# A four-layer macaron network: layer 1 as one run over the token chunks, and row sums by chunk

## The chip, the core and the metric

One Trainium2 chip, one NeuronCore. The metric is the device time of one execution in microseconds (us), the median of several runs. Instructions run on five engines that take their own queues in order: PE (TensorE matmul), DVE (VectorE), ACT (ScalarE), POOL (GpSimd) and SP (SyncE, which here issues DMAs). All arithmetic is float32.

## What is computed

The input x has B = 2 rows of S = 512 tokens with D = 256 features. Four layers follow each other, and each is a half-weighted FFN, an attention-like mixer and the same half-weighted FFN again. `LN` is a layer norm without weights.

```
for L in (0, 1, 2, 3):
    x = x + 0.5 * ffn_L(LN(x))
    x = x + attn_L(LN(x))
    x = x + 0.5 * ffn_L(LN(x))
```

The FFNs of layers 0 and 3 are mixtures of experts (layer 0 picks 6 of 32 for each token). Layer 1's FFN is one 256 x 256 product with a binarized weight and a bias. Layer 1's mixer is a sparse attention with 16 heads of 16:

```
importance = x @ Wi + bi                    # one number for each token
mask = (importance > its 103rd largest in the row) or (token is among the 32 most important)
q = x @ Wq + bq;  k = (x @ Wk + bk) * mask;  v = (x @ Wv + bv) * mask
out = softmax(q k^T / 4) v,  then  out @ Wo + bo
```

Layer 0's mixer is a retention network, and those of layers 2 and 3 are state-space (Mamba) blocks.

## The kernel before

The 1024 tokens are NC = 8 chunks of P = 128. x stays in SBUF for the whole program as `self.x[:, c, :]`, 128 tokens by 256 features a chunk; chunks 0 to 3 are row b = 0, chunks 4 to 7 row b = 1 (CB = 4 chunks a row). KD = 2 is the number of 128-feature halves. A product needs tokens along the free axis, so each norm ends in PE transposes through PSUM and a copy by DVE or ACT.

**Order.** Most stages are plain loops whose instructions a scheduler then places on each engine; the order on an engine is fixed before the program runs. In the Mamba blocks `in_order` (near L140) ties the instructions of PE, ACT and DVE to the order in which the code calls the pieces.

**Sums that are left over.** A mixture of experts writes each token's K expert outputs to a DRAM array and does not add them itself. `add_rows` (L637 to L651) brings them back, a pair of chunks in one `y2` buffer, and adds: for K = 6 one DVE addition of 128x768 (L648) and three of 128x256 (L651). It is stored as `pending[b]`, and whoever reads x first calls `settle(b)` (L155), which adds all four chunks of the row. `moments(b)` (L172 to L179) calls it and then takes mean and variance of the four chunks on DVE (`bn_stats` L178, `bn_aggr` L179). `scales` (L184 to L188) makes 1/sqrt(var + eps) for four chunks on POOL: an addition (L187) and a power (L188), each on a 128x4 tile. `layernorm` (L193) applies it on DVE, chunk by chunk.

**Layer 0's mixer** (the loop that begins at L978): eight chunks go through a software pipeline, `norm`, `project`, `turn`, `scores`, `values` and so on. `scales(b)` there (L735 to L743) makes two factors for a row by two powers of 128x4.

**Layer 1** is three stages.

- `l1_ffn` (L1030 to L1045), for each row: `row(b)` norms and transposes the row, DVE adds the bias (L1038, 128x1024), PE makes `ps_y` (L1042, two matmuls of 128x256 a chunk), and DVE adds it to x (L1045).
- `l1_attn`: POOL makes the tables `before` (L1081, used to break ties between ranks), `weight` (L1095, L1096) and clears `va` (L1100). `norm(0)`, `importance(0)` (`ib`, L1119), `ranks` (L1134 to L1140), `places` (L1145 to L1149), `norm(1)`, then keys and values of the picked tokens. Then comes a loop over n = 0 to 15 half-chunks: `scores` (PE `ps_s` L1253; DVE `mx` L1257 and `p` L1259; ACT's exponential L1260), `turn` (PE transposes `ps_t` L1268), `values` (PE `po` L1281), `finish` (`pt_o` L1295, `den`, `o`), and `project` (PE `pt2` L1309, ACT copy `oT2` L1311, POOL adds the bias `bo` to x L1313, PE `pw` L1316, DVE adds `pw` to x L1317). The loop's PSUM pool `a1n` has one buffer of each tag; `pt2` and `pw` share the tag `mm`.
- `l1_ffn` again for both rows.

**The Mamba blocks** (`mamba`, L1840 ff. for the opening that the change touches) begin with `row(0)`, the decay sums `d0`, `d1` (`pd`, `dt`, `dA`, `ps_row`, `cr`), the convolution's taps on DVE (L1584) and the `silu` on ACT (L1588), then the first chunks' exponents.

Of the kernel before, what the change touches and what calls it, by code (L numbers as in the profile page):

```python
# [32 lines left out]
def _const_array():  # L33
# [11 lines left out]
        "icol": np.arange(NC)[None, :] * P + p,  # L45
        "own": (p // 16 % 2 == np.arange(2)[None, :]),
# [33 lines left out]
class Net:  # L80
# [74 lines left out]
    def settle(self, b):  # L155
        if b in self.pending:
            self.pending.pop(b)()
# [6 lines left out]
    def transpose_tokens(self, src, dst, psum, half, k):  # L164

        ps = psum.tile([P, S], F32, tag="mm", name="ps_tr")
        for j in range(CB):
            self.nc.tensor.transpose(ps[:, j * P : (j + 1) * P], src[:, j, k * P : (k + 1) * P], self.ident)  # L168
        self.evac(dst[:, k, half * S : (half + 1) * S], ps)

# [32 lines left out]
    def layernorm_T(self, es, psum):  # L203
# [16 lines left out]
        def row(b):  # L220
            measure(b)
            norm(b)
            for k in range(KD):
                turn(b, k)

# [344 lines left out]
    def moe(self, pre, names, E, F, K, FS, PER, tiles, cap, r, scores, scale):  # L570
# [69 lines left out]
        def add_rows(b):  # L640
            for c0 in range(b * CB, (b + 1) * CB, 2):
                y2 = self.w("y2")[:, : 2 * K * D].rearrange("p (c n d) -> p c n d", c=2, n=K)
                for i in range(2):
                    nc.sync.dma_start(y2[:, i], rv[c0 + i, :, :K, :])
                for i in range(2):
                    y, xc, n = y2[:, i], self.x[:, c0 + i, :], K
                    if n == 6:
                        nc.vector.tensor_tensor(y[:, 0:3], y[:, 0:3], y[:, 3:6], ALU.add)  # L648
                        n = 3
                    for j in range(n):  # L650
                        nc.vector.tensor_tensor(xc, xc, y[:, j], ALU.add)  # L651

        for b in range(B):
            self.pending[b] = partial(add_rows, b)
# [49 lines left out]
    def l0_attn(self):  # L704
# [10 lines left out]
        with ExitStack() as es:  # L715
# [14 lines left out]
            rstd = sb.tile([P, NC], F32, name="ln_rstd")  # L730
            rr = sb.tile([P, NC], F32, name="ln_rr")
# [3 lines left out]
            def scales(b):  # L735
                bs = slice(b * CB, (b + 1) * CB)
                mv = mvs[b] = self.moments(sb, b)
                var = mv[:, :, 1]
                nc.gpsimd.tensor_scalar(rr[:, bs], var, 1.0 + EPS, EPS * EPS, ALU.mult, ALU.add)
                nc.gpsimd.tensor_tensor(rr[:, bs], rr[:, bs], half[:, :CB], ALU.pow)  # L740
                nc.gpsimd.tensor_scalar(rstd[:, bs], var, EPS, None, ALU.add)
                nc.gpsimd.tensor_tensor(rstd[:, bs], rstd[:, bs], half[:, :CB], ALU.pow)
                nc.vector.scalar_tensor_tensor(nb[:, bs], mv[:, :, 0], -1.0, rstd[:, bs], ALU.mult, ALU.mult)  # L743
# [16 lines left out]
            def norm(c):  # L760
                hn = wk.tile([P, D], F32, tag="hn", name="hn")
                nc.vector.tensor_scalar(
                    hn, self.x[:, c, :], mvs[c // CB][:, c % CB, 0:1], rr[:, c : c + 1], ALU.subtract, ALU.mult
                )
                nc.scalar.activation(
                    h0[:, c, :], self.x[:, c, :], AF.Identity, bias=nb[:, c : c + 1], scale=rstd[:, c : c + 1]
# [204 lines left out]
            scales(0)  # L971
            norm(0)
            scales(1)
# [4 lines left out]
            for s in range(NC + 4):  # L978
                if 0 <= s - 2 < NC:
                    scores(s - 2)  # L980
                if s + 1 < NC:
                    norm(s + 1)
# [23 lines left out]
    def l1_ffn_ahead(self):  # L1006
# [3 lines left out]
        self.hb = self.row("L1_ffn_bias")  # L1010
        with tc.tile_pool(name="f1p", bufs=1) as sb, tc.tile_pool(name="f1pm", bufs=2, space=PSUM) as psM:
# [18 lines left out]
    def l1_ffn(self):  # L1030
        nc, tc = self.nc, self.tc
        with ExitStack() as es:
            psM = es.enter_context(tc.tile_pool(name="f1m", bufs=8, space=PSUM))
            xT, row, measure, norm, turn = self.layernorm_T(es, psM)
            for b in range(B):
                row(b)
                xb = self.x[:, b * CB : (b + 1) * CB, :]
                nc.vector.tensor_tensor(xb, xb, self.hb.unsqueeze(1).to_broadcast([P, CB, D]), ALU.add)  # L1038
                for c in range(b * CB, (b + 1) * CB):
                    ps = psM.tile([P, D], F32, tag="mm", name="ps_y")  # L1040
                    for k in range(KD):
                        nc.tensor.matmul(  # L1042
                            ps, xT[:, k, c * P : (c + 1) * P], self.bwT[:, k, :], start=(k == 0), stop=(k == KD - 1)
                        )
                    nc.vector.tensor_tensor(self.x[:, c, :], self.x[:, c, :], ps, ALU.add)  # L1045


    def l1_attn(self):
# [15 lines left out]
        with ExitStack() as es:  # L1064
# [4 lines left out]
            wt = self.w("w4")[:, : KD * 4 * D].rearrange("p (k n d) -> p k n d", k=KD, n=4)  # L1069
            for n, name in enumerate(("Wq", "Wk", "Wv", "Wo")):  # L1070
                nc.sync.dma_start(wt[:, :, n, :], a[pre + name].rearrange("(k p) d -> p k d", p=P))
            wi = sb.tile([P, KD, 1], F32, name="wi")
            nc.sync.dma_start(wi, a[pre + "Wi"].rearrange("(k p) o -> p k o", p=P))
            bq, bk = self.col(pre + "bq", D), self.col(pre + "bk", D)
            bv, bo, bi = self.row(pre + "bv"), self.row(pre + "bo"), self.row(pre + "bi", 1)
            wib = sb.tile([P, KD, P], F32, name="wib")
            nc.gpsimd.tensor_copy(wib, wi.to_broadcast([P, KD, P]))

            before = sb.tile([P, CB, S], F32, name="before")
            for cc in range(CB):  # L1080
                nc.gpsimd.tensor_scalar(  # L1081
                    before[:, cc, :], self.c["jrow"], self.c["icol"][:, cc : cc + 1], None, ALU.is_lt
                )
# [9 lines left out]

            weight = sb.tile([P, 1], F32, name="weight")
            nc.gpsimd.tensor_scalar(weight, self.c["icol"][:, 0:1], P - 1.0, float(S - P), ALU.is_equal, ALU.mult)  # L1095
            nc.gpsimd.tensor_scalar(weight, weight, 1.0, None, ALU.add)  # L1096
            vas, kbs, ibs = [], [], {}
            for b in range(B):
                vas.append(sb.tile([P, NH, HQ], F32, name=f"va{b}"))
                nc.gpsimd.memset(vas[b], 0.0)  # L1100
                nc.gpsimd.tensor_copy(vas[b][:, :, DH : DH + 1], weight.unsqueeze(1).to_broadcast([P, NH, 1]))
                kbs.append(sb.tile([P, KD, 2, P], F32, name=f"kb{b}"))

            def norm(b):
                xr = xn[:, b * CB : (b + 1) * CB, :]
                self.layernorm(sb, xr, b, *self.scales(sb, b))
                for k in range(KD):
                    self.transpose_tokens(xr, xT, psM, b, k)
# [20 lines left out]
            def ranks(b, cc):  # L1129
# [8 lines left out]
                nc.vector.scalar_tensor_tensor(t, ib, me, before[:, cc, :], ALU.is_equal, ALU.mult)  # L1138
# [88 lines left out]
            bqs = sb.tile([P, KD], F32, name="bqs")  # L1227
            nc.vector.tensor_scalar(bqs, bq, DH**-0.5, None, ALU.mult)
            with tc.tile_pool(name="a1m", bufs=4, space=PSUM) as psM:
                norm(0)  # L1230
                importance(0)
                for cc in range(CB):
                    ranks(0, cc)
# [230 lines left out]
    def mamba(self, pre, win, wout, nh):  # L1464
# [14 lines left out]
        with ExitStack() as es:  # L1479
# [359 lines left out]
            with self.in_order(tail, ("PE", "Activation", "DVE")):  # L1839
# [6 lines left out]
                if few:  # L1846
                    measure(1)
# [174 lines left out]
```

## Time and profile before

| what | value |
|---|---|
| median of 3 runs | 2051.31 us (2039.61 to 2053.77) |
| the profiled execution's own time | 2134.34 us |
| its span, first to last instruction | 2132.1 us, mean granted PE clock 0.901 |
| busy share of the span | PE 83%, DVE 54%, POOL 41%, ACT 37% |
| layer 1 in the span | about 740 to 925 us |

The stages found from the timeline, in us from the start of the span: layer 0's first FFN to 288, its mixer to 455, its second FFN to 735; layer 1 to 925; layer 2 to 1240; layer 3 from there, with its mixer's sums read in from 1358 and its second FFN from 1993, to 2132. The page's list of costly groups is led by the experts and the Mamba blocks, which the change does not enter; so this case is read by windows and by the timeline, not by the list. In a timeline line the columns are the start in us, the time in us, the engine, line, operation and tiles, how many instructions the line holds, and in brackets how long the engine had been idle and what ended that.

### The profile page before, as it was taken

The numbers are of one execution on the slowest core, as the hardware profiler recorded it, in microseconds if no ns is written. First come the engines' busy times: TensorE is split into PE (matmuls) and PEld (weight loads), VectorE is DVE, ScalarE is ACT, GpSimd is POOL, SyncE is SP. The second block draws the span as 40 slices with busy tenths as digits, with TensorE's granted clock in tenths as the row PEclk, the third lists the DMA queues.
The fourth block names the chain that finished last, engine by engine and source line by source line (L and its number), as shares of the span: only waits on it lengthen the run. The fifth ranks groups of instructions, "written<-read, shape, count | busy, mean of one in ns | idle before, by whom it ended". The sixth has DMA issues, their size and how long they took to land. (4 is left out here: it accounts for less than half of the span.)

```text
span 2132.1 us, 29472 instructions
## 1 busy us (share of the span) xinstructions
PE 1772.7 (83%) x10590; PEld 1258.1 (59%) x10590; DVE 1144.8 (54%) x2679; ACT 798.5 (37%) x1329; POOL 879.1 (41%) x821
## 2 busy tenths in 40 slices
PE   6898849898888737879687988569999999999885
PEld 4576626565666524554366456447777677777564
DVE  5432256316322268656564653377777767776533
ACT  1122214311122204510562012267877677777111
POOL 3466545330666430000042016124566537667253
PEclk8999969998999858979697989789999999999788
DMA  8255450040455340000221013243444444544132
GB/s 286 78 163 157 138 207 12 1 149 24 137 163 159 115 173 1 1 21 0 90 91 31 10 30 96 95 133 119 154 148 149 159 137 154 165 142 128 41 92 91
DMA packets 117438, 226.00 MB, mean 106 GB/s; under 512 B 22382, under 2 KB 68828, under 8 KB 117142
## 3 DMA queue, kind: packets, MB, share of 16 engines
q1 hardware_dynamic: 88134, 170.17, 24.6%
q0 software_dynamic: 20608, 48.45, 7.0%
q10 hardware_dynamic: 8528, 5.26, 0.8%
q8 instruction: 92, 1.51, 0.3%
q14 instruction: 76, 0.62, 0.1%
HBM read 195.13 MB, written 41.81 MB: 111 GB/s over the span
## 5 line engine op out<-in xcount | busy, mean ns | idle before, releaser
L475 POOL DMA_INDIRECT xe<-table,sl_get x176 | 179.8, 1022 | 228.5 <-DVE sl_get L451 146.7
L499 PE MATMUL ps_gu<-we,xeT 128*128 128x352 f32 x704 | 238.1, 481 | 0.0
L529 POOL DMA_INDIRECT rows<-ye,sl_put x176 | 177.0, 1005 | 139.7 <-ACT ye L128 45.6
L524 PE MATMUL ps_ye<-we,hT 88*128 88x256 f32 x704 | 178.6, 396 | 40.7 <-issue 14.1
L1584 DVE SCALAR_TENSOR_TENSOR xc<-pp,L_attn_cols,xc 128x511 f32<-128x511 f32 (+2 forms) x216 | 161.4, 747 | 48.5 <-ACT xc L1580 43.2
L524 PEld LDWEIGHTS ps_ye<-we,hT 88*128 88x128 f32 x704 | 134.7, 195 | 86.7 <-issue 19.6
L504 DVE SCALAR_TENSOR_TENSOR he<-se,xe,ps_gu 128x176 f32<-128x176 f32 x176 | 68.4, 396 | 208.4 <-issue 106.7
L499 PEld LDWEIGHTS ps_gu<-we,xeT 128*128 128x128 f32 x704 | 133.8, 202 | 59.3 <-issue 10.3
L187 POOL TENSOR_SCALAR ln_rstd<-ln_mv 128x4 f32<-128x4 f32 x22 | 5.1, 234 | 393.9 <-DVE ln_mv L179 389.4
L1711 PE MATMUL pz<-xT,wt 128*128 128x128 f32 x1152 | 145.1, 280 | 19.5 <-DVE state L1758 8.0
L1687 DVE SCALAR_TENSOR_TENSOR lm<-lm,jb,top 128x128 f32<-128x128 f32 x576 | 153.6, 340 | 0.0
L1711 PEld LDWEIGHTS pz<-xT,wt 128*128 128x128 f32 x1152 | 137.7, 195 | 25.2 <-issue 9.3
L1577 PE MATMUL pp<-xT,wx 128*128 128x512 f32 x288 | 145.2, 629 | 1.5 <-ACT dec L1568 0.9
L1784 PE MATMUL yacc<-wt,y 128*128 128x256 f32 x576 | 144.1, 393 | 0.7 <-POOL y L1766 0.7
L1766 POOL TENSOR_TENSOR y<-y,sg 128x512 f32<-128x512 f32 x72 | 91.7, 1274 | 108.4 <-DVE y L1765 107.1
L1704 POOL TENSOR_TENSOR ce<-ce,CT 128x1024 f32<-128x1024 f32 x54 | 128.0, 2370 | 0.0
L128 ACT COPY xT<-ps_tr 128x512 f32<-128x512 f32 x22 | 12.8, 584 | 293.4 <-PE ps_tr L168 264.9
L503 ACT ACTIVATE se<-ps_gu 128x176 f32<-128x176 f32 x176 | 54.7, 318 | 172.9 <-PE ps_gu L499 75.8
L1784 PEld LDWEIGHTS yacc<-wt,y 128*128 128x128 f32 x576 | 104.6, 191 | 24.1 <-issue 10.6
L1416 PE MATMUL ps_y<-w8T,xT 128*128 128x512 f32 x256 | 118.5, 617 | 0.0
L1739 PE MATMUL py<-lm,xt 128*64 128x128 f32 x1152 | 109.2, 284 | 6.2 <-issue 5.4
L168 PE MATMUL ps_tr<-cst,xn 128*128 128x128 f32 x176 | 41.9, 394 | 86.5 <-DVE xn L193 67.0
(383 smaller groups left out, 3552.4 us busy)
## 6 DMA issues: line engine op xcount, KB each, us to landing
lm<-rows SPq DMA_DIRECT2D x72, 512.0 KB
ce<-rows SPq DMA_DIRECT2D x54, 512.0 KB
rows<-zero POOLq DMA_DIRECT2D x16, 768.0 KB
y<-rows SPq DMA_DIRECT2D x16, 768.0 KB
we<-in_L_ffn_w_gate_dram SPq DMA_DIRECT2D x64, 176.0 KB
we<-in_L_ffn_w_up_dram SPq DMA_DIRECT2D x64, 176.0 KB
we<-in_L_ffn_w_down_dram SPq DMA_DIRECT2D x64, 176.0 KB
we<-in_L_ffn_w_dram SPq DMA_DIRECT2D x48, 176.0 KB
```

What stands on the lines that cost most here:

```text
L475: nc.gpsimd.indirect_dma_start(xe[:, i, :], None, table, bass.IndirectOffsetOnAxis(get[:, e * per + j : e * per + j + 1], 0), bounds_check ...
L499: nc.tensor.matmul(pg, xeT[:, k, i * P : (i + 1) * P], wgu[:, :, k], start=(k == 0), stop=(k == KD - 1))
L524: nc.tensor.matmul(py[:, i, :], hT[:, q, i * P : (i + 1) * P], wd[:, q, :], start=(q == 0), stop=(q == 1))
L529: put_rows = nc.gpsimd.indirect_dma_start(rows, bass.IndirectOffsetOnAxis(put[:, e * per + j : e * per + j + 1], 0), y[:, i, :], None, bou ...
L1416: nc.tensor.matmul(ps, xT[:, k, cs], self.w8T[:, k, 2 * e2 : 2 * e2 + 2, :], start=(k == 0), stop=(k == KD - 1))
L1577: nc.tensor.matmul(pp, wv[:, k, :], xT[:, k, b * S : (b + 1) * S], start=(k == 0), stop=(k == KD - 1))
L1584: nc.vector.scalar_tensor_tensor(out[:, 3 - w :], pp[:, : S - 3 + w], cw[:, m, w : w + 1], out[:, 3 - w :], ALU.mult, ALU.add)
L1687: nc.vector.scalar_tensor_tensor(k["lm"][:, h, :], k["lm"][:, h, :], jb[:, k["c"], n : n + 1], top, ALU.add, ALU.min)
L1704: nc.gpsimd.tensor_tensor(k["ce"], k["ce"], ct, ALU.mult)
L1711: nc.tensor.matmul(pz[:, m, :], u["wz"][:, kk, m * P : (m + 1) * P], xT[:, kk, c * P : (c + 1) * P], start=(kk == 0), stop=(kk == KD - 1),)
L1739: nc.tensor.matmul(py[i * HP : (i + 1) * HP, m, :], w[:, h * HP : (h + 1) * HP], v[:, h, :], start=(m == 0 and n == 0), stop=(n == len(src ...
L1784: nc.tensor.matmul(yacc[cc // 2][:, cc % 2, :], k["y"][:, m, :], u["wo"][:, m, :], start=(u["g"] == 0 and m == 0 and cc % 2 == 0), stop=(u ...
```

## The change

1. **Sums by chunk.** `pending[b]` is a list of four parts, and `settle(b, n)` adds the first n of them. The first part issues the DMAs of all four chunks. If a PSUM pool is handed over, a chunk's six pieces are added by six PE products with the identity into `ps_add`, and DVE adds that once.
2. **Layer 0's mixer** makes its factors by chunk (`scales(c)`), two chunks ahead of the loop, with one power of 128x2 instead of two of 128x4. The rest are made in the loop.
3. **Layer 1 is one function `l1`.** A first loop takes chunk c through `front` (sum, mean and variance, power of 128x1), chunk c-1 through `turn_x` (norm, transposes, ACT copy, bias on POOL), c-2 through `back` (the FFN's product and addition), c-3 through `measure` and c-4 through attention's `norm` (whose POOL part now adds `bo`). `importance(0)`, `queries(0)` and `ranks(0)` follow in its last steps. In the attention loop, `front`, `turn_x` and `back` of the second FFN run some steps behind `project`, in the same one-buffer PSUM tag `mm`. `before` and `weight` become columns of the constants array that is loaded at the start, and Layer 1's small vectors are loaded ahead, in layer 0.
4. **The Mamba openings**: `row(b)` of a row with sums still to add goes chunk by chunk (`by_chunks`); the calls of `d0`, `d1`, the taps and `silu` of the first units stand in another order; in layer 3 the norm of row 1 comes one step later.
5. **The store** adds a chunk's sums ahead of that chunk's DMA.

```diff
-        def add_rows(b):
...
+        def add_rows(b, cc, psum):
+            c, pair = b * CB + cc, cc // 2
+            if cc == 0:
...
+            if psum:
+                ps = psum.tile([P, D], F32, tag="mm", name="ps_add")
+                for j in range(n):
+                    nc.tensor.matmul(ps, self.ident, y[:, j], start=(j == 0), stop=(j == n - 1))
+                nc.vector.tensor_tensor(xc, xc, ps, ALU.add)
+                return
...
+    def scale(self, pool, name, c):
+        mv = self.moment(pool, name, c)
+        rstd = pool.tile([P, 1], F32, name=f"ln_rs{name}")
+        nc.gpsimd.tensor_scalar(rstd, mv[:, 1:2], EPS, None, ALU.add)
+        nc.gpsimd.tensor_tensor(rstd, rstd, self.mhalf[:, 0:1], ALU.pow)
+        return mv, rstd
...
+            def front(c):
+                self.settle(c // CB, c % CB + 1, psM if c % 2 or c >= CB else None)
+                ms[c] = self.scale(sb, f"{nth}_{c}", c)
+            def turn_x(c):
+                fx = self.centre(sb.tile([P, D], F32, tag="fxn", name="fxn", bufs=3), c, *ms.pop(c))
+                pt = psM.tile([P, KD, P], F32, tag="mm", name="pt")
+                for k in range(KD):
+                    nc.tensor.transpose(pt[:, k, :], fx[:, k * P : (k + 1) * P], self.ident)
+                xts[c] = sb.tile([P, KD, P], F32, tag="fxT", name="fxT", bufs=3)
+                nc.scalar.copy(xts[c], pt)
+                nc.gpsimd.tensor_tensor(self.x[:, c, :], self.x[:, c, :], self.hb, ALU.add)
+            def back(c):
+                xT = xts.pop(c)
+                ps = psM.tile([P, D], F32, tag="mm", name="ps_y")
+                for k in range(KD):
+                    nc.tensor.matmul(ps, xT[:, k, :], self.bwT[:, k, :], start=(k == 0), stop=(k == KD - 1))
+                nc.vector.tensor_tensor(self.x[:, c, :], self.x[:, c, :], ps, ALU.add)
...
             with tc.tile_pool(name="a1m", bufs=4, space=PSUM) as psM:
-                norm(0)
-                importance(0)
-                for cc in range(CB):
-                    ranks(0, cc)
+                for c in range(NC + 4):
+                    if c < NC:
+                        front(c)
...
+                    if 0 <= c - 1 < NC:
+                        turn_x(c - 1)
+                    if 0 <= c - 2 < NC:
+                        back(c - 2)
+                    if 0 <= c - 3 < NC:
+                        measure(c - 3)
+                    if c >= 4:
+                        norm(c - 4)
...
                 if n >= 4 and n % 2 == 0 and (n - 4) // 2 < NC:
                     project((n - 4) // 2)
+                if n >= 5 and n % 2:
+                    if (n - 5) // 2 < NC:
+                        front((n - 5) // 2)
+                    if 0 <= (n - 7) // 2 < NC:
+                        turn_x((n - 7) // 2)
+                if n >= 8 and n % 2 == 0 and (n - 8) // 2 < NC:
+                    back((n - 8) // 2)
...
                 exponents(ks[0])
                 x[2][0]()
+                x[2][1]()
...
                 raised(ks[0])
-                x[2][1]()
```

## The prediction

> **What bounds the kernel now.** I read the page first. PE leads:
>
> ```profile
> PE 1772.7 (83%) x10590; PEld 1258.1 (59%) x10590; DVE 1144.8 (54%) x2679; ACT 798.5 (37%) x1329; POOL 879.1 (41%) x821
> ```
>
> An average of 83% says nothing of the stages that the change touches, so I cut the span into windows around them. Columns: length, then busy us (instructions) of PE, PE's weight loads, DVE, ACT and POOL, the granted PE clock, the DMA share, GB/s. The windows are the opening of layer 0's mixer, its steps, layer 1's first FFN, its attention steps and its second FFN.
>
> ```profile
> 290.00:305.00 15.00, 0.00 (x0) 0.00 (x0) 11.59 (x27) 0.00 (x0) 4.53 (x13) 0.50 1.00 389
> 305.00:455.00 150.00, 130.27 (x960) 84.41 (x961) 70.48 (x183) 52.88 (x128) 73.34 (x80) 0.92 0.18 60
> 745.00:785.00 40.00, 16.93 (x48) 12.59 (x48) 29.13 (x70) 1.17 (x2) 3.35 (x5) 0.56 0.67 241
> 843.00:901.00 58.00, 50.18 (x502) 32.82 (x502) 38.72 (x52) 33.42 (x53) 0.00 (x0) 0.97 0.01 1
> 901.00:926.00 25.00, 15.18 (x62) 11.77 (x62) 17.50 (x57) 1.83 (x4) 3.79 (x6) 0.80 0.13 43
> ```
>
> Both FFNs of layer 1 leave PE idle about half the time, at a clock of 0.56 in the first; attention's steps keep it 87% busy. What PE waits for stands in the timeline of DVE:
>
> ```profile
> 794.29 2.20 DVE L193 TENSOR_SCALAR xn<-x,ln_mv,ln_rstd 128x256 f32<-128x256 f32 x4 [6.66 <-POOL ln_rstd L188]
> ...
> 801.43 0.74 DVE L1119 TENSOR_SCALAR ib<-pb,row_L_attn_bi 128x512 f32<-128x512 f32 x1
> ...
> 825.57 1.22 DVE L1257 TENSOR_REDUCE mx<-ps_s 128x8 f32<-128x1024 f32 x1
> ...
> 867.69 0.42 DVE L1317 TENSOR_TENSOR x<-x,pw 128x256 f32<-128x256 f32 x1 [1.24 <-PE pw L1316]
> ...
> 875.75 0.42 DVE L1317 TENSOR_TENSOR x<-x,pw 128x256 f32<-128x256 f32 x1 [1.23 <-PE pw L1316]
> ...
> 924.27 0.41 DVE L1045 TENSOR_TENSOR x<-x,ps_y 128x256 f32<-128x256 f32 x1
> ```
>
> The first importance comes at 801.43, 56.5 us after the first sum (744.98); the first scores at 825.57; a chunk of attention takes 8.06 us; the second FFN ends 19.3 us after the last `pw` (905.42). The 6.66 us idle is POOL, which builds a table before it takes the norm:
>
> ```profile
> 784.31 6.19 POOL L1081 TENSOR_SCALAR before<-cst 128x512 f32<-128x512 f32 x4 [10.23 <-PE ps_y L1042]
> ...
> 793.22 1.04 POOL L188 TENSOR_TENSOR ln_rstd<-ln_rstd,mhalf 128x4 f32<-128x4 f32 x1
> ```
>
> The openings of layers 0, 3 and 2 have the same look: first norm after all four chunks' sums (layer 0's first sum was at 292.84, layer 3's sums ended at 1365.15), and PE without work behind ACT:
>
> ```profile
> 307.59 0.41 DVE L762 TENSOR_SCALAR hn<-x,ln_mv,ln_rr 128x256 f32<-128x256 f32 x1
> ...
> 1369.09 1.38 DVE L193 TENSOR_SCALAR xn<-x,ln_mv,ln_rstd 128x256 f32<-128x256 f32 x4 [1.54 <-POOL ln_rstd L188]
> ```
> ```profile
> 1062.17 1.11 PE L1659 MATMUL pt<-cst,xc 128*128 128x128 f32 x4 [10.23 <-ACT xc L1588]
> ```
>
> **What the Trainium skill says.** "Perfetto Trace Analysis", Optimizing Scalar/DVE Operations: if those engines aren't saturated but cause bubbles elsewhere, breaking up instructions may let work finish sooner. That is this change, and DVE at 54% with PE waiting fits. "GPSIMD Engine Reference", 4.1: GpSimd is about twice as slow as VectorE for a two-input operation; the trace has `bo`'s addition at 0.74 us on POOL against 0.42 on DVE. "TensorE: Matmul & The Clock Gate", Part 1: the array runs at half rate unless it has been busy; 16 matmuls of `ps_y` took 6.64 us at 777 and 3.72 us at 920, so 0.42 against 0.23 each. "ScalarE: Activation LUTs", What ACT_TABLE_LOAD costs: about 1.28 us and a drain; the trace shows the 1.28.
>
> **The change part by part**, against the profiled execution (2134.3 us; the runs' median is 3.9% lower, so the sum is scaled by 0.961 at the end).
>
> *Front of layer 1.* The y pieces arrive 2.1 us apart as before. In the steady step DVE does: add `ps_add` 0.42, statistics 0.43, aggregate 0.17, add `ps_y` 0.42, norm 0.35, statistics 0.43, aggregate 0.17, norm 0.35 = 2.74. Each norm waits for POOL's addition 0.22 and power. No 128x1 power is in the trace. I split 1.04 for 128x4 into 0.22 fixed and 0.205 a column: 0.42 (bounds 0.22 and 1.04). With handoffs of 0.2 a wait is 0.84; the first is half covered by adding `ps_y` (0.42 left), the second is open and has 0.2 more, because POOL first adds the FFN's bias (0.73). Step 2.74 + 0.42 + 1.04, and 0.15 for POOL's `bo`: 4.4 us. PE fits beside it: six identity products at the cold 0.42 are 2.5, transposes and `ps_y` some 1.9. The first norm is at about 749.3 (744.98, sum 2.3, statistics 0.6, wait 0.84, and the next chunk's work between); 7.4 steps later, at 782, stands importance: -19.4. With a power of 1.04 the step is 5.6, and it is -11. The table on POOL is gone. From importance to the first scores it was 24.1, and stays that and 0.7 for chunk 7's leftovers: first scores 807, -18.7.
>
> *Attention's steps.* The chunk is a ring: `x+=pw`, `mx`, `p`, exponential, `ps_t`, `po`, `pt2`, `pw`. DVE's queue now has, between `x+=pw` and the next `mx`, statistics 0.43, aggregate 0.17, the wait 0.84, norm 0.35, and `ps_y` 0.42, less the overlaps in the trace: `mx` starts 2.75 after `x+=pw` instead of 0.67. Behind them stand `mx`, and PE's `ps_t`. So +2.05 a chunk, six chunks, less in the first two: +11.6; +3.6 more at 1.04. The two small PE pieces (transposes 0.44, `ps_y` 0.5) run in the time that `mx` is awaited; without that cover they cost about 1 a chunk.
>
> *Second FFN.* 19.3 us after the last `pw` become 4.8 (one norm, transposes, copy, product, addition), and 1.3 for the last `pw`: -13.2.
>
> Layer 1: -18.7 + 11.6 - 13.2 = -20.3. Bounds: -7 (power 1.04), -25 (0.22).
>
> *Layer 0's mixer.* Chunk 0's mean and variance are there at 296.9 as before (its sum, statistics and aggregate behind 292.84); POOL then needs 0.32 + 0.23 for two additions and, by my split, 0.63 for one power of two columns: first norm at 298.2, not 307.59: -9.4. The remaining sums, 2.3 each, go into steps where DVE is 47% busy; a part will be late. The second row's y DMAs move on SP behind `fc1` and `fc2`, needed only four steps on. I take -7.5 (0 to -9.4).
>
> *Mamba openings.* Layer 3: statistics and norm of three chunks go under the sums; first transposes done about 3.4 earlier, and `cr` before the taps. Layer 2: one 1.28 table load less on ACT, the bubble of 10.23 shrinks. Bounds 0 and -5 for layer 2, +2 and -8 for layer 3 (its row 1 norm is a step later); I take -3 and -5.
>
> *Start.* The constants grow from 717 KB by 897 columns, 448 KB, beside x's load at about 385 GB/s: +1.2, as the first statistics wait for x (8.30). Ahead loads of small vectors: nothing, hidden under layer 0's experts. *Store*: the same order as before, 0.
>
> Sum: -20.3 - 7.5 - 3 - 5 + 1.2 = -34.6; times 0.961, -33: 2018 us.
>
> **Rivals.**
>
> *A: the power does not shrink with its columns* (a 128x1 costs 1.04). [...] Against: additions of 128x4 and 128x1 (0.22 to 0.25) show a small fixed part. Layer 1 gives -7, the sum is -21: 2031.
>
> *B: gains outside layer 1 are swallowed.* PE is 87% busy in layer 0's steps, and the Mamba loop is bound elsewhere; the early start may only move a wait. Layer 1 alone with the start: -19 x 0.961, 2033.
>
> *C, the other side: the one-buffer tag `mm` paces attention.* Four tiles a chunk (`pt2`, `pw`, `pt`, `ps_y`) take turns in it, and each is freed by DVE or ACT from their queues. If each turn takes a half-step of 4.03, a chunk takes 16.1, +8.06 a chunk instead of 2.05, +64 for +11.6: the total is +18, 2069. All gains (-46 without the steps' own cost) are used up when a chunk takes 13.8 us (46 / 8 over 8.06). Against: the ring's own work is 4.0 with eight handoffs of 0.2, below 8.06, so most turns hide.
>
> *D: the front's loop is slower than its queues say*, PE at half clock and DVE in turn, 7 us a step: layer 1 about 0, total -15: 2037.
>
> **How the numbers follow.** Forecast 0.57, A 0.13, B 0.12, D 0.10, C 0.08. The likeliest case alone is 2006 to 2028. The range takes in A, B and D and leaves C and the tails: 1998 to 2044. About 1% (20.5 us, below 2031 or above 2072) is what a measurement of this kernel can tell from no change; the forecast lies almost wholly beyond, A and B on the edge, D within: faster 0.72, same 0.21, slower 0.07 (C and wider).
>
> **What would show it.** First importance about 37 us after the first sum (56.5 before); POOL's power of 128x1 near 0.42; chunks of attention near 10.1 us; under 6.5 us from the last `pw` to the last `ps_y`; layer 0's first norm about 5.4 us after its first sum (14.75 before). The forecast is wrong if chunks take over 12, or if a step of the front takes over 6.

## The result, and the profile after

The changed kernel takes 2029.85 us (median of 9 runs, 2027.53 to 2035.52); nine runs of the kernel before on the same chip have a median of 2048.94 (2039.61 to 2053.77). The ratio is 0.9917, 95% interval [0.9898, 0.9935]: 17 us faster, within 13 to 21. That is inside the predicted range and beyond doubt a gain, but half the 33 us of the forecast, and within the 1% that the prediction counted as the same.

The page's first line after the change:

```profile
PE 1762.7 (87%) x10662; PEld 1259.7 (62%) x10662; DVE 1131.6 (56%) x2657; ACT 800.6 (39%) x1342; POOL 903.5 (45%) x889
```

The span is 2028.0 us. It is not set against the 2132.1 of before, since that execution, like all runs beside the experiment e12 below, took some 4% longer than the others, with its first layer-0 sum at 292.84 (e12: 290.74) where the rest have 254 to 257. I compare stage by stage, each from its own first instruction. The windows that answer to those of before (same columns): layer 0's opening, its steps, layer 1's front, its attention steps, and what is left behind them.

```profile
252.00:267.00 15.00, 1.55 (x5) 1.11 (x6) 9.24 (x21) 1.99 (x5) 8.10 (x20) 0.50 1.02 378
267.00:417.00 150.00, 130.27 (x953) 84.37 (x952) 72.91 (x195) 50.33 (x124) 74.16 (x89) 0.94 0.18 58
681.00:721.00 40.00, 31.14 (x128) 25.05 (x129) 23.24 (x64) 4.84 (x13) 20.79 (x42) 0.84 0.70 245
771.00:838.00 67.00, 57.68 (x487) 36.60 (x486) 42.93 (x71) 31.61 (x54) 9.31 (x19) 0.95 0.00 1
838.00:853.00 15.00, 9.05 (x29) 4.96 (x27) 4.23 (x12) 1.49 (x4) 2.82 (x6) 0.77 0.00 1
```

Layer 1's front now keeps PE 78% busy at a clock of 0.84, where the first FFN had 42% at 0.56. The attention steps are as dense as before (86%) but last longer. Layer 0's 150 us of steps look alike. DVE's timeline gives the milestones of layer 1:

```profile
681.32 0.96 DVE L711 TENSOR_TENSOR y<-y 128x768 f32<-128x768 f32 x1 [2.14 <-DMA y<-rows]
...
718.03 0.41 DVE L198 TENSOR_SCALAR fxn<-x,ln_mv,ln_rs 128x256 f32<-128x256 f32 x1 [0.69 <-POOL ln_rs L194]
...
723.47 0.75 DVE L1185 TENSOR_SCALAR ib<-pb,row_L_attn_bi 128x512 f32<-128x512 f32 x1 [0.52 <-PE pb L1181]
...
749.92 1.21 DVE L1348 TENSOR_REDUCE mx<-ps_s 128x8 f32<-128x1024 f32 x1
...
806.18 0.42 DVE L1407 TENSOR_TENSOR x<-x,pw 128x256 f32<-128x256 f32 x1 [1.44 <-PE pw L1406]
808.28 0.41 DVE L198 TENSOR_SCALAR fxn<-x,ln_mv,ln_rs 128x256 f32<-128x256 f32 x1 [1.00 <-POOL ln_rs L194]
...
808.94 1.22 DVE L1348 TENSOR_REDUCE mx<-ps_s 128x8 f32<-128x1024 f32 x1
...
816.31 0.42 DVE L1407 TENSOR_TENSOR x<-x,pw 128x256 f32<-128x256 f32 x1 [1.44 <-PE pw L1406]
...
842.51 0.42 DVE L1407 TENSOR_TENSOR x<-x,pw 128x256 f32<-128x256 f32 x1 [2.46 <-PE pw L1406]
...
852.28 0.42 DVE L1163 TENSOR_TENSOR x<-x,ps_y 128x256 f32<-128x256 f32 x1 [3.44 <-PE ps_y L1162]
```

The two milestones of before that the prediction gives without their lines are the first sum and the last `pw`:

```profile
744.98 0.96 DVE L648 TENSOR_TENSOR y<-y 128x768 f32<-128x768 f32 x1 [9.66 <-DMA y<-rows]
...
905.00 0.42 DVE L1317 TENSOR_TENSOR x<-x,pw 128x256 f32<-128x256 f32 x1 [2.25 <-PE pw L1316]
```

A chunk of attention is 816.31 - 806.18 = 10.13 us (8.06 before), and `mx` starts 2.76 after `x+=pw`, with a 1.00 us wait for POOL's addition and power in between. In numbers, each row a difference of two such starts or ends:

| stage, us | before | after |
|---|---|---|
| layer 1: first sum to importance | 56.5 | 42.2 |
| importance to the first scores' `mx` | 24.1 | 26.5 |
| `mx` to the last `pw` added | 79.9 | 93.0 |
| last `pw` to the last `ps_y` added | 19.3 | 9.8 |
| layer 1 in all | 179.7 | 171.4 |
| layer 0's mixer: first sum to first norm | 14.8 | 5.9 |
| layer 0's mixer: first sum to last addition | 183.6 | 184.9 |
| layer 2: first FFN to its last addition / from there to the first Mamba `y` | 87.9 / 58.6 | 89.8 / 55.5 |
| layer 3: first sum to first `y` | 60.7 | 59.1 |
| layer 3: first to ninth Mamba `y` | 81.7 | 72.1 |

The differences add up to -8.3 + 1.3 + 1.9 - 3.1 - 1.6 - 9.6 = -19.4, within the interval of the runs. So in these two traces layer 1 brought less than half of its -20.3, layer 0 nothing, and layer 3 the most, in a stretch where the prediction had priced the edit (row 1's norm a step later) as a possible loss. The experiments ask three things: what of layer 1's steps and tail ate its gain, where layer 0's 9 us went, and whether the shifted norm is really what layer 3 gained from.

### The profile page after: what moved, and what is told of

Same layout as the page of the kernel before. It is cut to its first block, busy times and chain, and to the rows that moved or that the text cites. A ratio compares the mean times of both kernels' runs of the same rounds, so it can differ in the third digit from the quotient of the medians.

```text
span 2028.0 us, 29711 instructions
## 1 busy us (share of the span) xinstructions
PE 1762.7 (87%) x10662; PEld 1259.7 (62%) x10662; DVE 1131.6 (56%) x2657; ACT 800.6 (39%) x1342; POOL 903.5 (45%) x889
## 5 line engine op out<-in xcount | busy, mean ns | idle before, releaser
L551 PE MATMUL ps_gu<-we,xeT 128*128 128x352 f32 x704 | 232.5, 472 | 0.0
L1682 DVE SCALAR_TENSOR_TENSOR xc<-pp,L_attn_cols,xc 128x511 f32<-128x511 f32 (+2 forms) x216 | 161.4, 747 | 34.7 <-ACT xc L1678 29.4
L576 PE MATMUL ps_ye<-we,hT 88*128 88x256 f32 x704 | 168.3, 379 | 2.9 <-ACT ye L132 1.6
L551 PEld LDWEIGHTS ps_gu<-we,xeT 128*128 128x128 f32 x704 | 130.0, 196 | 56.5 <-issue 5.5
L1882 PEld LDWEIGHTS yacc<-wt,y 128*128 128x128 f32 x576 | 104.8, 191 | 24.2 <-issue 10.8
L1875 POOL TENSOR_TENSOR sqs<-sqs,sq 128x512 f32<-128x512 f32 x56 | 71.4, 1275 | 89.4 <-ACT sq L1874 89.4
L1794 DVE TENSOR_TENSOR lm<-lm,M 128x1024 f32<-128x1024 f32 x72 | 87.1, 1215 | 42.7 <-ACT lm L1790 41.1
```

Source lines behind the costliest of these rows:

```text
L551: nc.tensor.matmul(pg, xeT[:, k, i * P : (i + 1) * P], wgu[:, :, k], start=(k == 0), stop=(k == KD - 1))
L576: nc.tensor.matmul(py[:, i, :], hT[:, q, i * P : (i + 1) * P], wd[:, q, :], start=(q == 0), stop=(q == 1))
L1682: nc.vector.scalar_tensor_tensor(out[:, 3 - w :], pp[:, : S - 3 + w], cw[:, m, w : w + 1], out[:, 3 - w :], ALU.mult, ALU.add)
L1882: nc.tensor.matmul(yacc[cc // 2][:, cc % 2, :], k["y"][:, m, :], u["wo"][:, m, :], start=(u["g"] == 0 and m == 0 and cc % 2 == 0), stop=(u ...
```

## The experiments

**The two halves.** The first (e1) has layer 1's function alone, with layer 0's `scales(b)`, the Mamba openings, their `parts` and `row(b)` as before; the second (e2) has layer 1's three stages `l1_ffn`, `l1_attn`, `l1_ffn` with their tables and the small array of constants as before, and all the rest as after.

> Only layer 1's part of the change; the openings of layer 0's mixer and of the two Mamba blocks are those of before. Theory (read from the two traces): layer 1 takes 171.4 us instead of 179.7, so about 8 us faster than before (ratio 0.996). Rival (the step sum of the prediction held and the profile misleads): 19 us faster (0.991).

> The whole change but layer 1, whose three stages are those of before. Theory: the openings of layers 2 and 3 give some 3 and 2 us, layer 0's mixer nothing although its first norm is 9 us earlier: about 5 us faster than before (0.9975), and with e1 the whole 19 us is not explained. Rival: layer 0's mixer does give its 7.5: 13 to 15 us faster (0.993).

Layer 1 alone: 2033.82 us, ratio 0.9934 [0.9921, 0.9947]. All but it: 2043.71, 0.9977 [0.9965, 0.9989]. The gains of 0.66% and 0.23% add up to about the 0.83% of both. In the traces layer 1 takes 170.5 us with its edit and 180.1 without, so this stage's gain is not an accident of the one profile of before.

The runs share the gain out differently from the table, though: 13.5 us (10.9 to 16.2) for layer 1's edit and 4.7 (2.3 to 7.2) for all else, where the table has 8.3 for layer 1 and 11.2 for layer 3. What lies between is in stages that differ from kernel to kernel with the same code in them. From layer 2's last `y` to layer 3's first sum it is 206.4 to 214.6 us in all traces but those of before and e12. Layer 2's opening, up to its first `y`, takes one of two times: 55.0 to 55.5 in six traces with the reordered calls and 57.9 to 59.2 in six others (e2, e3, e4, e6, e8, e12), and without them 58.6 (before) and 54.9 (e1). e9 and e12 have the same code there and in layer 1, and 55.5 and 59.2. So the table's -3.1 in layer 2 can be put down neither to the reordered calls nor to layer 1's edit, and parts of the table under some 4 us are not resolved.

**Attention's steps: is it the position of the second FFN in DVE's queue?** The scheduler puts statistics, norm and `ps_y` between `x+=pw` and the next `mx`. My theory was that the order of the code, tied on DVE, would put the norm where POOL's power is done and bring chunks back towards 8 us. Three kernels: DVE tied in the attention loop (e3); tied in the front's loop too (e4); and tied with the pieces called later, the norm behind the scores (e8).

```diff
 e3:
+            with self.in_order({}, ("DVE",)):
                 for n in range(N + 9):
 e4: the same, and around the front's loop
+                with self.in_order({}, ("DVE",)):
                     for c in range(NC + 4):
 e8: as e3, with turn_x and back after scores(n), front last
+                    if n >= 7 and n % 2 and (n - 7) // 2 < NC:
+                        back((n - 7) // 2)
+                    if n >= 6 and n % 2 == 0 and (n - 6) // 2 < NC:
+                        turn_x((n - 6) // 2)
```

> The changed kernel, with DVE tied to the order of the code in layer 1's attention loop: the norm of a chunk for the second FFN then stands a whole chunk behind its own statistics. Theory: the 2.07 us that a chunk grew is DVE waiting for POOL's power in front of the next scores; the interval of pw falls from 10.13 to about 8.5, 10 to 13 us faster than after. Rival (the one-buffer tag mm or PE paces the chunk): the interval stays near 10.

> As e3, and the first loop of layer 1 in the order of the code too. Theory: a step of the front falls from 4.51 us to about 3.3 (POOL's own work), and importance comes about 5 us earlier than in e3, less one or two steps of a deeper pipeline. Rival: POOL's queue was the bound of the front anyway, and nothing comes of it beyond e3.

> The changed kernel; layer 1's attention loop has DVE in the order of the code, and the code puts the second FFN's norm behind the scores of the next half-chunk and its product's addition behind the scores after that, so neither POOL's power nor the turn of the one-buffer tag stands ahead of a chunk's scores. Theory (the ring from x+=pw to mx is what grew; e3 only traded POOL's wait for the tag's): pw interval 9 us or less instead of 10.13, and 5 to 12 us faster than after. Rival: the four turns in the tag pace the chunk whatever DVE's order, interval 10 or more.

The ratios are 0.9949 [0.9935, 0.9962], 1.0069 [1.0053, 1.0085] and 0.9990 [0.9977, 1.0003]: none better than the scheduler's order. DVE's timeline of the first:

```profile
809.49 0.42 DVE L1407 TENSOR_TENSOR x<-x,pw 128x256 f32<-128x256 f32 x1 [1.50 <-PE pw L1406]
...
811.25 0.42 DVE L1163 TENSOR_TENSOR x<-x,ps_y 128x256 f32<-128x256 f32 x1 [1.34 <-PE ps_y L1162]
```

The wait for POOL is gone, and in its place DVE waits 1.34 us for `ps_y`. PE can begin that only when `x+=pw` has freed the one buffer of `mm` (it starts at 810.01, 0.10 after that addition's end), and it is now asked for at once. The chunk takes 10.8. With the pieces late (e8) it takes 10.73 and the first one 18.6, with 3.1 to 4.3 us of DVE idle before each `x+=pw` but the first: the scheduler has put the next scores' products (823.26 to 825.88) on PE ahead of `pw` (826.04). In the front (e4), tied DVE and PE take turns: PE's six identity products of one chunk stand at 712.30, behind transposes for which PE had waited 1.44 for DVE's norm; they take 5.33 us at a granted clock of 0.50, DVE's addition waits 5.90 for them, and first sum to importance takes 68.0. My theory fell: moved, the wait comes back as another. What the second FFN adds to the ring stays in these three orders; e3's order with a PSUM buffer of its own for `ps_y` was not run.

**Is POOL's power in the ring?** One more 128x1 power a chunk, on a scratch tile, ahead of the real one (second FFN only).

```diff
+        nc.gpsimd.tensor_tensor(more, rstd, self.mhalf[:, 0:1], ALU.pow)
         nc.gpsimd.tensor_tensor(rstd, rstd, self.mhalf[:, 0:1], ALU.pow)
```

> The changed kernel with one more power of 128x1 on POOL, on a tile that nobody reads, ahead of the power of each chunk of the second FFN. Theory: POOL's power stands in the ring of the attention steps, so each chunk takes another 0.57 to 0.65 us and the interval of pw goes from 10.13 to about 10.75, 4 to 5 us slower than after in all. Rival (the turns in the tag mm pace the chunk, and POOL's wait lies beside them): intervals unchanged.

Measured 2040.44 us, 0.9971 [0.9957, 0.9984]. DVE's timeline of it:

```profile
809.13 0.42 DVE L1410 TENSOR_TENSOR x<-x,pw 128x256 f32<-128x256 f32 x1 [1.44 <-PE pw L1409]
...
811.86 0.41 DVE L201 TENSOR_SCALAR fxn<-x,ln_mv,ln_rs 128x256 f32<-128x256 f32 x1 [1.63 <-POOL ln_rs L197]
...
819.89 0.42 DVE L1410 TENSOR_TENSOR x<-x,pw 128x256 f32<-128x256 f32 x1 [1.44 <-PE pw L1409]
```

The wait grows from 1.00 to 1.63 and the chunk from 10.13 to 10.76: the whole 0.63 us shows in the ring. The first two and the last two intervals grow by more (1.3 to 2.2 us), and layer 1 takes 180.7, 9 us more than after, twice what I expected; the runs are slower by as much. So POOL's power is on the path.

**What do the steps cost against what they hide?** The second FFN out of the steps, by row behind the loop as the kernel before had it; the rest as after.

```diff
-            for n in range(N + 9):
+            for n in range(N + 6):
...
-                if n >= 5 and n % 2:
-                    if (n - 5) // 2 < NC:
-                        front((n - 5) // 2)
-                    if 0 <= (n - 7) // 2 < NC:
-                        turn_x((n - 7) // 2)
-                if n >= 8 and n % 2 == 0 and (n - 8) // 2 < NC:
-                    back((n - 8) // 2)
...
-    "l1",
+    "l1", "l1_ffn",
```

> The changed kernel, with layer 1's second FFN taken out of the attention steps and run after them for a row at a time, as before. Theory: in the steps it costs 13.2 us (93.0 against 79.8 from the first scores to the last pw) and saves 9.5 behind them, so taking it out gives 3 to 4 us: intervals of pw back at 8.06, 19.3 us after the last pw, about 4 us faster than after. Rival: the front's new order has changed the steps, and the intervals stay above 9.

Measured 2023.91 us, 0.9884 [0.9863, 0.9904], the fastest kernel of this study. DVE's timeline:

```profile
798.43 0.42 DVE L1428 TENSOR_TENSOR x<-x,pw 128x256 f32<-128x256 f32 x1 [1.23 <-PE pw L1427]
...
806.49 0.42 DVE L1428 TENSOR_TENSOR x<-x,pw 128x256 f32<-128x256 f32 x1 [1.23 <-PE pw L1427]
```

The chunk is 8.06 again, the stretch from `mx` to the last `pw` 78.8, and the tail 19.1. Layer 1 takes 166.0 against 171.4 after: in the steps the second FFN costs 14.2 us, and it saves 9.3 behind them. That half of the edit loses 5 us in the traces (the two ratios' intervals, 0.9863 to 0.9904 and 0.9898 to 0.9935, overlap by 0.0006), and the other half, the front, carries the whole gain of layer 1.

**The tail.** Behind the last `pw` remain 9.8 us and not 4.8. The theory: chunks 6 and 7 take turns in `mm`. The last two chunks' tiles get the tags `t0` and `t1`, whose users are done by then.

```diff
+                if nth and c >= NC - 2:
+                    pt = psM.tile([P, NQ, P], F32, tag="t0", name="pt")[:, :KD, :]
...
+                if nth and c >= NC - 3:
+                    ps = psM.tile([P, NQ, P], F32, tag="t1", name="ps_y")[:, :KD, :].rearrange("p k n -> p (k n)")
```

> The changed kernel; the tiles of the second FFN's last two chunks (and the product of the third last) take the PSUM tags t0 and t1, which are idle by then, instead of mm. Theory: behind the last pw it took 9.8 us and not the 4.8 predicted, because the last chunks' transposes and products take turns in the one buffer mm; this brings it to 5 to 6.5 us, 3 to 4 us faster than after. Rival: the chain of norm, copy and product of two chunks takes 9 us anyway.

DVE's timeline, from the last `pw` to the last `ps_y`:

```profile
843.54 0.42 DVE L1413 TENSOR_TENSOR x<-x,pw 128x256 f32<-128x256 f32 x1 [0.79 <-PE pw L1412]
...
849.83 0.42 DVE L1169 TENSOR_TENSOR x<-x,ps_y 128x256 f32<-128x256 f32 x1 [3.43 <-PE ps_y L1168]
```

850.25 - 843.96 = 6.3 us, so the shared buffer is worth 3.5 of the 5 us in the trace. From `mx` to the last `pw` it took 0.5 us more (93.5), and the runs (2030.65, 0.9918 [0.9899, 0.9937]) don't resolve what is left.

**Layer 0's mixer.** Three kernels: its scales by row with two powers of 128x4, as before (e5); the product `nb`, before which DVE waits for POOL, moved to POOL (e6); and, on top of e9, six of its eight chunk sums made on PE (e12), to see whether DVE's sums are the bound.

```diff
 e6:
-                nc.vector.scalar_tensor_tensor(
-                    nb[:, c : c + 1], mv[:, 0:1], -1.0, sc[:, c, 1:2], ALU.mult, ALU.mult
-                )
+                nc.gpsimd.tensor_scalar(nb[:, c : c + 1], mv[:, 0:1], sc[:, c, 1:2], -1.0, ALU.mult, ALU.mult)
 e12: e9 and
-                self.settle(c // CB, c % CB + 1)
+                self.settle(c // CB, c % CB + 1, psM if c % 2 or c >= CB else None)
```

> The changed kernel with layer 0's mixer as before (factors for a row at a time, all sums ahead of the loop). Theory, from the traces of e1 and after: the part lost 3.5 us (181.4 against 184.9 from the first sum to the last addition), so this is some 3.5 us faster than after. Rival: the 8.9 us earlier first norm pays somewhere, and it is 5 to 8 us slower than after.

> The changed kernel; in layer 0's mixer the small product nb = -mean * rstd goes to POOL instead of DVE, nothing else. Theory: DVE waits 1.2 to 1.4 us for POOL at nb of each of the eight chunks, with the steps' other work queued behind it, and that ate the early start; with nb on POOL the wait only stands at the norm itself, a step later for the last four chunks: 2 to 5 us faster than after. Rival: the later sums on DVE (2.3 us each, inside the steps) are what is late; then no change within 1 us.

> e9, and layer 0's mixer sums six of its eight chunks on PE, as layer 1's front does, instead of on DVE. Theory: the first norm 8.9 us earlier brought nothing because DVE is the bound of that mixer's first 45 us (77% busy with a sum of 2.3 us a chunk and waits for POOL), so moving six sums off DVE, 1.9 us each, makes chunk 5's norm some 8 to 11 us earlier and the whole 5 to 9 us faster than e9. Rival: PE or the clock at half rate bounds that stretch, the added products cost what they save, and it equals e9.

With the scales by row: 2028.85 us, 0.9897 [0.9872, 0.9921], not told from the changed kernel's 0.9917. The stage took 185.3 us there and 181.4 in e1, which has the same order in it, so some 4 us of this stage vary between programs for other reasons; the 3.5 us that I expected can't be resolved, and layer 0's edit is worth 0 within 4. If anything it costs: e1, which has layer 0 and the openings as before, is 0.28% (5.7 us) faster than e7 below, and both lack the shift in layer 3. With `nb` on POOL: 2032.09, 0.9907 [0.9888, 0.9927], no change; where DVE waited for POOL at `nb` (1.17 to 1.41 us) it now waits as long at the first four `hn`. With six sums on PE: 2116.16 where the kernel before has 2126.03, 0.9939 [0.9917, 0.9961]; only the stage is read. The windows 15 to 45 us behind the first sum, of the changed kernel:

```profile
270.00:285.00 15.00, 12.51 (x74) 6.67 (x72) 10.73 (x22) 6.70 (x17) 7.83 (x11) 1.00 0.29 106
285.00:300.00 15.00, 12.92 (x125) 8.53 (x126) 13.72 (x38) 4.75 (x12) 7.08 (x10) 0.89 0.23 73
```

and of e12, 17 to 47 us behind it:

```profile
308.00:323.00 15.00, 14.51 (x90) 10.13 (x89) 8.64 (x19) 4.61 (x13) 5.11 (x8) 1.00 0.29 106
323.00:338.00 15.00, 15.00 (x148) 10.04 (x147) 8.25 (x25) 5.16 (x14) 8.38 (x12) 1.00 0.22 73
```

In the changed kernel DVE is 82% busy in those 30 us and PE 85%. With the sums on PE, DVE falls to 56% and PE is full (98%). Chunk 5's norm then comes 51.9 us after the first sum instead of 54.5, but the last addition at 186.9 instead of 184.7 (e9). So the sums on PE cost there what they save on DVE, as the rival had it; that DVE's work alone holds chunk 5's norm back in the changed kernel is not shown.

**Layer 3's shifted norm.** One step undone in the changed kernel:

```diff
-                    parts = [lambda: measure(1), None, lambda: norm(1), lambda: turn(1, 0), lambda: turn(1, 1)]
+                    parts = [lambda: measure(1), lambda: norm(1), lambda: turn(1, 0), lambda: turn(1, 1)]
```

> The changed kernel, but in layer 3's mixer the norm of row 1 follows its statistics in the next step, as before, instead of two steps on. Theory: the first eight steps of the Mamba loop took 72.1 us against 80.8, because DVE no longer waits for POOL's queue of long multiplications at that norm; undone, 5 to 8 us slower than after. Rival: the order of the opening (cr and dA earlier) made it, and this is equal to after.

Measured 2040.47 us, 0.9962 [0.9947, 0.9976]: 9 us slower than after by the ratios and 10.6 by the medians, and the first eight `y` intervals take 80.9 us instead of 72.1 (e1, without the shift too: 80.8; e2, with it: 72.1). DVE's timeline without the shift:

```profile
1352.15 0.41 DVE L223 TENSOR_SCALAR xn<-x,ln_mv,ln_rstd 128x256 f32<-128x256 f32 x1
1352.47 1.35 DVE L223 TENSOR_SCALAR xn<-x,ln_mv,ln_rstd 128x256 f32<-128x256 f32 x1
1353.74 1.13 DVE L223 TENSOR_SCALAR xn<-x,ln_mv,ln_rstd 128x256 f32<-128x256 f32 x1
1354.79 2.44 DVE L223 TENSOR_SCALAR xn<-x,ln_mv,ln_rstd 128x256 f32<-128x256 f32 x1
1357.15 0.68 DVE L1856 TENSOR_TENSOR state<-state,pst 128x512 f32<-128x512 f32 x1
...
1363.47 0.69 DVE L1863 TENSOR_TENSOR y<-xc,py 128x512 f32<-128x512 f32 x1 [1.16 <-PE py L1837]
```

POOL in the same stretch:

```profile
1352.37 1.30 POOL L1864 TENSOR_TENSOR y<-y,sg 128x512 f32<-128x512 f32 x1 [1.27 <-DVE y L1863]
1353.64 1.09 POOL L1825 TENSOR_TENSOR xd<-xt,dec 128x512 f32<-128x512 f32 x1
1354.68 2.40 POOL L1802 TENSOR_TENSOR ce<-ce,CT 128x1024 f32<-128x1024 f32 x1
```

PE, behind them:

```profile
1357.88 3.56 PE L1809 MATMUL pz<-xT,wt 128*128 128x128 f32 x16 [3.70 <-DVE state L1856]
```

and DVE with the shift (the changed kernel):

```profile
1352.15 0.68 DVE L1856 TENSOR_TENSOR state<-state,pst 128x512 f32<-128x512 f32 x1
...
1360.20 0.68 DVE L1863 TENSOR_TENSOR y<-xc,py 128x512 f32<-128x512 f32 x1
1360.80 2.33 DVE L223 TENSOR_SCALAR xn<-x,ln_mv,ln_rstd 128x256 f32<-128x256 f32 x4
```

Without the shift the four norms stand ahead of `state`, the Mamba loop's own work, and take 5.09 us in all, where four norms undisturbed take 1.38 (layer 3's first row before: 0.41 each, overlapping). The mean of 1.27 hides what happens. The first starts before POOL's product and takes 0.41; each of the other three starts while a two-input product of POOL runs and ends 0.15 us after it (1353.67, 1354.73 and 1357.08), so it takes as long as that product has left. PE waits 3.70 us for `state` behind them. With the shift they come behind the `y`, and of the 2.33 us one norm beside POOL's product makes 1.36. So DVE did not wait in front of the norm for POOL's queue, as I had expected; the norm itself was drawn out. The next `y` is at 1363.47 against 1360.20: 3.3 us in this step, with both traces alike up to 1352.15. The other 5 to 6 us come in two later steps, where row 1's transposes also move by one; those I did not take apart.

## Why the prediction was right or wrong

**Front of layer 1: right in kind, -14.3 instead of -19.4.** The step was priced at 4.4 us and is 4.51. The number of steps was the wrong term: from the first norm to importance it is 38.1 us, 8.45 steps and not 7.4. Importance stands 5.4 us behind the eighth norm, and the first three steps take 4.87 each at a mean granted clock of 0.75. "PE fits beside it: six identity products at the cold 0.42 are 2.5" was also wrong. PE's timeline after:

```profile
707.38 2.86 PE L707 MATMUL ps_add<-y,cst 128*128 128x256 f32 x12 [0.35 <-DVE x L708]
...
718.50 0.44 PE L1153 MATMUL pt<-cst,fxn 128*128 128x128 f32 x2 [2.45 <-DVE fxn L198]
...
719.86 3.58 PE L1181 MATMUL pb<-xT,wib 128*128 128x512 f32 x4
```

A chunk's six products are twelve instructions: 2.86 us at the full clock, 5.33 at half (e4). In a step (704.49 to 709.00) PE is busy 4.16 of 4.51 us, so it is nearly as full as DVE's queue with its waits. The last lines show why importance is late: its product `pb` needs the four chunks of row 0 alone, whose last transposes stand at 715.67, but on PE it comes behind chunk 7's, for which PE waits 2.45 us. What an earlier place would give was not run.

**POOL's power: between the bounds, nearer the middle than I took.** The view of the tile `ln_rs` on POOL:

```profile
L194 POOL TENSOR_TENSOR ln_rs<-ln_rs,mhalf x20: 567/568/726, 684.7 to 1290.5; 128x1 f32<-128x1 f32 x20
```

0.568 us, not 0.42 (bounds 0.22 and 1.04), so the wait is 1.00 and not 0.84. Layer 0's power of 128x2 takes 0.720 and the old one of 128x4 takes 1.036. The three lie on a line, 0.41 us fixed and 0.157 a column: the split was right in form, but an addition's 0.22 was the wrong fixed part.

**Importance to the first scores: +2.3, not +0.7.** Of the growth, 2.0 lies ahead of row 1's importance (15.2 us behind row 0's, 13.2 before): chunk 7's norm comes at 732.66 on DVE, behind row 0's ranks, and PE waits 5.04 us for it. So chunk 7's leftovers cost more than I put.

**Attention's steps: right, the sum partly by luck.** +13.2 us (93.0 - 79.9) against 11.6 + 1.3 = 12.9, a chunk of 10.13 against "near 10.1", `mx` 2.76 after `x+=pw` against 2.75. The mechanism holds (e11), but the sum fits better than its parts: the first two intervals grew by 3.2 each (13.1 and 11.3) where the prediction had less than 2.05, the later ones by 1.3 to 2.1, and from `mx` to the first `pw` it took 2.4 less than before (21.7 against 24.2). The advice to break up instructions, which the prediction took for the whole change, paid in the front, where PE was 42% busy. In the steps PE was already 87% busy and the ring closed, and there it cost 14.2 us for 9.3 (e9).

**Second FFN behind the steps: -9.5, not -14.5** (the -13.2 of the sum holds 1.3 for the last `pw`, counted with the steps here). The sum had one chunk's chain, 4.8 us. Left over are two chunks that take turns in `mm`, 9.8 us; with other buffers 6.3 (e10). The prediction named this tag as rival C for the pace of the steps, where the changed kernel's DVE shows no wait for it, and left it out of the tail, where it decides.

Layer 1 in all: -8.3 in the profiles (-9.6 from e2 to e1) instead of -20.3. Of the 12 us that are missing in the profiles, 5.1 are the front's, 5.0 the tail's, 1.6 stand between importance and scores, and 0.3 in the steps.

**Layer 0's mixer: the failed step.** DVE's timeline has the first norm 5.9 us after the first sum (5.4 forecast), and chunk 5's where it was:

```profile
260.68 0.41 DVE L825 TENSOR_SCALAR hn<-x,ln_mv,ln_sc 128x256 f32<-128x256 f32 x1
...
309.10 0.41 DVE L825 TENSOR_SCALAR hn<-x,ln_mv,ln_sc 128x256 f32<-128x256 f32 x1
```

309.10 is 54.3 us after the first sum (254.80). Before:

```profile
292.84 0.96 DVE L648 TENSOR_TENSOR y<-y 128x768 f32<-128x768 f32 x1 [14.67 <-DMA y<-rows]
...
346.80 0.41 DVE L762 TENSOR_SCALAR hn<-x,ln_mv,ln_rr 128x256 f32<-128x256 f32 x1
```

That is 54.0. "The remaining sums, 2.3 each, go into steps where DVE is 47% busy" took an average over 150 us for the steps that the sums must go into: 9.24, 10.73 and 13.72 of three 15 us windows, 75%, are the opening. From 252 to 417 PE stood idle 165 - 1.55 - 130.27 = 33.2 us, and in the 165 us of before (290 to 455) 34.7: the idle time only moved. Rival B (a gain swallowed outside layer 1) held here. Which wait swallows it stays open: the sums on PE brought chunk 5's norm 2.6 us forward and the end none (e12).

**Mamba openings.** Layer 2: -1.2 net, not told from nothing, where -3 was forecast. Layer 3's opening: -1.6 with the reordered calls, against -5. Row 1's norm a step later: about -9, where the prediction had it as the reason for a bound of +2. The step that failed took a moved norm at its own length; what counted was what stands behind it in DVE's queue and what POOL does beside it. "GPSIMD Engine Reference", Key points, in the Trainium skill says that GpSimd contends with DVE instructions in a two-port mode, and "VectorE: DVE Perf Modes" there, Mode 2×_2P, names `tensor_scalar` on SBUF data as a user of that mode. The traces agree: 0.41 us alone, up to 2.44 beside POOL's two-input products. That the ports are the reason was not tested by itself.

Here the result owes something to luck: about 9 of its 17 us come from this norm, which the prediction had not counted as a gain. Without it the change measures 2040.47 (e7).

**Start, store, scale.** The +1.2 is there at the start: the first statistics, which wait for x, begin at 9.68 to 10.28 us in every kernel with the larger constants and at 8.28 and 8.30 in the two without (e2 and before). It is gone by layer 0's first sum, 254.1 to 257.0 with them (e12 apart) and 255.74 without (e2). The factor 0.961 had no ground: layer 1 takes 179.7 us in the profiled execution of before and 180.1 in e2, so what that execution lost lay outside the stages that change.

**The rivals.** A (power of 1.04) did not happen, nor C (16 us a chunk; it is 10.13), nor D (7 us a step; it is 4.5). B's time, 2033, is near the result by coincidence: layer 0 gave nothing, as it says, but layer 3's norm gave about 9 us and layer 1 less than B took. By its own step of 5.6, A's -11 for the front would be -10.

## What to carry to other kernels

Before work is put into a stage to hide it, ask for that stage's ring: a piece whose result another engine must hand back costs its work and its whole wait there, here 2.1 us a chunk, and leaving it behind the loop was 5 us cheaper. Cut windows as short as the moved work is long, since an average of 47% hid an opening at 75%, where a 9 us head start was worth nothing. When an instruction is moved, look at what runs beside it and what stands behind it in the new place, and take single instructions apart: a mean over four norms hid that three of them ended with another engine's work. Count the records that the trace shows for one call of the code.

## What the runs showed that I had not expected

A float32 product appears as two PE instructions (twelve for six products of 128x256, 2.86 us at the full clock), a transpose of 128x128 as one. POOL's power is 0.57 us for 128x1, 0.72 for 128x2 and 1.04 for 128x4: a fixed part and a small one for each column. DVE's 128x256 norm took 0.41 us alone, and 0.81 to 2.44 when it started beside a POOL addition or product of 128x256 to 128x1024 (before and e7), each time until 0.15 us after that instruction's end; beside POOL's power of 128x4 it kept its 0.41.
